# Four modulations computed as four strips of 32 columns, turned by sixteen small transfers

## The chip, the core and the metric

The kernel runs on one core of a Trainium2 chip. Such a core has five engines that run their own instruction streams and meet at semaphores: PE (matrix products; its weight loads are shown apart as PEld), DVE (VectorE), ACT (ScalarE), POOL (GpSimd) and SP (SyncE, which here only issues DMAs). Operands lie in SBUF (128 partitions); products come out in PSUM, used here as eight banks of 128 x 512 float32. The metric is the time of one execution in device microseconds, as a median over runs. All numbers are float32.

## What is computed

Two transformer layers, over 16 sequences of 256 tokens of width 256, with a conditioning vector per sequence. Each layer is self-attention, cross-attention to a context, and a feed-forward part:

```
layer 0 (16 heads of 64):
  adaln(x, g, b) = ln(x) * (1 + cond @ g) + cond @ b           # cond: 16 x 256
  x = attn(adaln(x, g1, b1)) + x                               # rotary positions
  x = cross_attn(adaln(x, g1, b1), ln(context)) + x
  x = gelu(adaln(x, g2, b2) @ ff_w1) @ ff_w2 + x
layer 1 (16 heads of 16):
  sh1, sc1, sh2, sc2, sh3, sc3 = split(silu(cond) @ Wmod, 6)
  x = x + attn(ln(x) * (1 + sc1) + sh1)
  x = x + cross_attn(ln(x) * (1 + sc2) + sh2, context)
  x = x + gelu((ln(x) * (1 + sc3) + sh3) @ W1) @ W2
```

A modulation is the pair of factors that scale and shift a normalised input: a product of 16 condition vectors (256 long) with a 256 x 512 weight, half of it the shift and half the scale. There are five: a1 (used by both attentions of layer 0), a2 (its feed-forward part), and b1, b2, b3 for the three parts of layer 1. The kernel wants each as a tile of 128 partitions (channel within a block of 128) by 2 (shift, scale) by 2 (block) by 16 (sequence), since it keeps activations with channels on partitions.

## The kernel before

The work is six phases (two attentions and a feed-forward part, for either layer) of 16 jobs, one per sequence. An attention job has two steps (s = 0, 1), a feed-forward job four. The order of instructions on every engine is the order in which the Python code emits them: nothing is rescheduled. A loop over all steps (from L901) emits, in each turn, pieces of the job at hand and of jobs ahead of it: normalisation three jobs ahead (`prepare_moments`, `prepare_norm`), the fetch of turned blocks two jobs ahead (`prepare_fetch`), the modulated input `hT` (`prepare_input`, L393 on ACT and L394 on POOL), the rotary products of the next step, and at the end of the turn the scores of the next step (`scores`, `stage_s`, L566).

PE products are mostly `product` (L80 to L82): four strips, each with 32 columns of weights and 32 partitions of output, one behind the other in the queue; the array holds the four side by side. In the trace a float32 product is two PE instructions.

One step of layer 0's cross-attention, with s = 1, matters below. DVE runs in this order: the moments of a later job at the end of the turn before (`context_moments`, its last instruction is L325); then `stage_t` twice (L587, sums of exponentials), `stage_turn` (L593), the rotary multiplications (L523, from PSUM) with `stage_t` between, `stage_reduce` (L600), and the additions of the finished output to x (`finish_folded`, L747 to L754, which read PSUM banks 4 and 5). POOL meanwhile runs `scale` (L624, four multiplications emitted at the end of step s = 0), `fold_inner` (L733), the rotary sums (L531). At the end of the turn PE computes the scores of the next step, first into banks 0 to 3, then into 4 to 7, so the second half has to wait until L754 has read bank 5.

There are two ways to compute a modulation. `modulation` (L180, used for a1 and a2) has the weights stationary: for each of 2 x 2 output blocks and each half of the inner dimension a product with 128 columns of weights and 16 columns streamed, whose result is already turned as it is wanted; five DVE instructions (`factors`, L173 to L177) make the factors from PSUM at once. For a2 this happens in job 2 of the cross-attention phase, at s = 1, between the first and second half of the rotary products. `modulation_turned` (L192, used for b1, b2, b3) has the 16 condition vectors stationary and streams 512 columns of weights, twice. The result has sequences on partitions. POOL clears a 32 x 512 tile (L202), ACT copies the result there (L203), DVE turns blocks of 32 x 32 (L205), SP moves the blocks to their partitions with four DMAs (L208), and `factors` runs later from SBUF. b1, b2 and b3 are made in jobs 2, 5 and 8 of layer 0's feed-forward phase at s = 3; their factors follow one job later (L931 to L933), at the head of step s = 3 of jobs 3, 6 and 9.

Of the kernel before, what the change touches and what calls it, by code (L numbers as in the profile page):

```python
# [10 lines left out]
F32 = mybir.dt.float32  # L11
# [5 lines left out]
P = 128  # L17
N = 256
D = 256
# [5 lines left out]
KC = D // P  # L25
# [18 lines left out]
def fast(ctx: ExitStack, tc: tile.TileContext, a: dict, out: bass.AP, flag):  # L44
# [4 lines left out]
    nc = tc.nc  # L49
    NB = a["x"].shape[0]  # L50
# [5 lines left out]
    work = ctx.enter_context(tc.tile_pool(name="work", bufs=2))  # L56
# [7 lines left out]
    def bank(i, *inner):  # L64

        flat = banks[:, i, :]
        if len(inner) == 1:
            return flat[:, 0 : inner[0]]
        return flat[:, 0 : inner[0] * inner[1]].rearrange("p (a n) -> p a n", n=inner[1])
# [34 lines left out]
    row_of, n_rows = {}, 0  # L104
# [20 lines left out]
    condT = const.tile([P, 2, KC, NB], F32, name="condT")  # L125
# [31 lines left out]
    def load_modulation(shift_w, scale_w, name, between=None):  # L157
        w = wpool.tile([P, KC, 2, D], F32, tag="mod", name=f"mod_{name}", bufs=1)
        nc.sync.dma_start(out=w[:, :, 0, :], in_=shift_w.rearrange("(c p) m -> p c m", p=P))
        if between is not None:  # L160
            between()
        nc.sync.dma_start(out=w[:, :, 1, :], in_=scale_w.rearrange("(c p) m -> p c m", p=P))
        return w

    def factors(name, pm, ln_w, ln_b, shift_b, scale_b):


        factor = stat.tile([P, KC, NB], F32, tag="fac", name=f"fac_{name}", bufs=4)
        addend = stat.tile([P, KC, NB], F32, tag="add", name=f"add_{name}", bufs=4)
        ln_w, ln_b, shift_b, scale_b = (  # L170
            cols[:, c : c + KC].unsqueeze(2).to_broadcast([P, KC, NB]) for c in (ln_w, ln_b, shift_b, scale_b)
        )
        nc.vector.tensor_tensor(addend, pm[:, 1], scale_b, ALU.add)  # L173
        nc.vector.scalar_tensor_tensor(factor, addend, 1.0, ln_w, ALU.add, ALU.mult)
        nc.vector.scalar_tensor_tensor(addend, addend, 1.0, ln_b, ALU.add, ALU.mult)
        nc.vector.tensor_tensor(addend, addend, shift_b, ALU.add)
        nc.vector.tensor_tensor(addend, pm[:, 0], addend, ALU.add)  # L177
        return factor, addend

    def modulation(name, at, w, *vectors):  # L180

        pm = bank(at, 2 * KC, NB).rearrange("p (s c) b -> p s c b", s=2)
        for s in range(2):
            for m in range(KC):
                for k in range(KC):
                    nc.tensor.matmul(
                        pm[:, s, m, :], w[:, k, s, m * P : (m + 1) * P], condT[:, 0, k, :],
                        start=(k == 0), stop=(k == KC - 1),
                    )
        return factors(name, pm, *vectors)  # L190

    def modulation_turned(name, at, w, *vectors):  # L192


        assert NB <= 32
        pm = bank(at, 2 * D)[0:NB]
        for k in range(KC):
            nc.tensor.matmul(
                pm, condT[:, 1, k, :], w[:, k].rearrange("p s m -> p (s m)"), start=(k == 0), stop=(k == KC - 1)
            )  # L200
        flat = work.tile([32, 2 * D], F32, tag="m0", name=f"flat_{name}")
        nc.gpsimd.memset(flat, 0.0)  # L202
        nc.scalar.copy(flat[0:NB], pm)  # L203
        blocks = work.tile([32, 2 * KC, 4, 32], F32, tag="m1", name=f"blocks_{name}")
        nc.vector.transpose(blocks.rearrange("p s q b -> p (s q b)"), flat)  # L205
        turned = work.tile([P, 2, KC, NB], F32, tag="inv", name=f"turned_{name}")
        for q in range(4):
            nc.sync.dma_start(  # L208
                out=turned[32 * q : 32 * q + 32].rearrange("p s c b -> p (s c) b"), in_=blocks[:, :, q, 0:NB]
            )  # L210
        return lambda: factors(name, turned, *vectors)

    def layer0_modulation(i, between=None):
        w = load_modulation(a[f"L0_xcond_b{i}_w"], a[f"L0_xcond_g{i}_w"], f"a{i}", between)
        return lambda at: modulation(
            f"a{i}", at, w,
            *(row_of[f"L0_xcond_{n}"][0] for n in (f"ln{i}_w", f"ln{i}_b", f"b{i}_b", f"g{i}_b")),
        )

    def layer1_modulation(i):  # L220
        at = 2 * (i - 1) * D
        w = load_modulation(
            a["L1_xcond_Wmod"][:, at : at + D], a["L1_xcond_Wmod"][:, at + D : at + 2 * D], f"b{i}"
        )
        c = row_of["L1_xcond_bmod"][0] + at // P
        return lambda at: modulation_turned(
            f"b{i}", at, w, row_of[f"L1_xcond_ln{i}_w"][0], row_of[f"L1_xcond_ln{i}_b"][0], c, c + KC
        )


# [559 lines left out]
    def count_outside():  # L790
# [10 lines left out]
    phases = [  # L801
        {"layer": 0, "kind": "attn", "cross": False, "load": lambda part: load_layer0_attention("sa", part, load_first),
         "mod_load": lambda: layer0_modulation(1, lambda: load_x(0))},
        {"layer": 0, "kind": "attn", "cross": True, "load": lambda part: load_layer0_attention("ca", part), "mod_load": None},
        {"layer": 0, "kind": "ffn", "cross": False, "mod_load": lambda: layer0_modulation(2),
         "load": lambda part: load_ffn("L0_xcond_ff_w1", "L0_xcond_ff_w2", "L0_xcond_ff_b1", "L0_xcond_ff_b2", "a", part)},
        {"layer": 1, "kind": "attn", "cross": False, "load": load_layer1_self, "mod_load": lambda: layer1_modulation(1)},
        {"layer": 1, "kind": "attn", "cross": True, "load": load_layer1_cross, "mod_load": lambda: layer1_modulation(2)},
        {"layer": 1, "kind": "ffn", "cross": False, "mod_load": lambda: layer1_modulation(3),
         "load": lambda part: load_ffn("L1_xcond_W1", "L1_xcond_W2", "L1_xcond_b1", "L1_xcond_b2", "b", part)},  # L810
    ]
# [18 lines left out]
    for p, ph in enumerate(phases):  # L830
        for b in range(NB):
            job = {"phase": ph, "p": p, "layer": ph["layer"], "kind": ph["kind"], "cross": ph["cross"], "b": b,
                   "key": f"{p}_{b}", "index": len(jobs), "qk": {}, "pr": {}, "turns": [], "raw": [], "parts": [], "halves": [],
                   "last": p == len(phases) - 1}
# [66 lines left out]
    for i, (j, s) in enumerate(steps):  # L901
        job = jobs[j]
        ffn, layer0 = job["kind"] == "ffn", job["layer"] == 0
# [17 lines left out]
            load_phase(job["p"] + 1, "first")  # L921
        if layer0 and not ffn and s == 1 and job["b"] == 2:
            make_mod = phases[job["p"] + 1]

        if ffn and layer0 and job["b"] in (2, 5, 8):
            at = phases[3 + job["b"] // 3]
# [4 lines left out]
        if ffn and layer0 and job["b"] in (3, 6, 9) and s == 3:  # L931
            at = phases[2 + job["b"] // 3]
# [84 lines left out]
        else:  # L1017
            then = attention(i + 1, 1)
            at = 4 * s
# [639 lines left out]
```

## Time and profile before

| | |
|---|---|
| median of 3 runs | 2198.77 us (2198.4 to 2199.13) |
| the profiled execution | 2198.01 us, of which its span is 2196.1 us |
| granted PE clock | 1.0 over the span |
| busy: PE, DVE, POOL, ACT | 2181.5, 1669.3, 1072.3, 838.2 us |
| sixteen PE instructions of a2 (L186) | 787.23 to 789.12 us |
| twelve PE instructions of b1, b2, b3 (L198), four each | the first starts at 1331.6, the last at 1414.4 us |

Busy time is the time in which an engine had an instruction of its own running; the rest of the span it waited. The chain of waits goes back from the last instruction to what released each, so a line of it is time that set the end. A timeline row gives start, length, engine, source line, operation and how many were merged; a bracket holds the idle time before it and what ended that. "SPq" rows are DMA issues: their length is the time that SP took to issue, not the transfer.

### The profile page before, as it was taken

The numbers are of one execution on the slowest core, as the hardware profiler recorded it, in microseconds if no ns is written. First come the engines' busy times: TensorE is split into PE (matmuls) and PEld (weight loads), VectorE is DVE, ScalarE is ACT, GpSimd is POOL, SyncE is SP. The second block draws the span as 40 slices with busy tenths as digits, with TensorE's granted clock in tenths as the row PEclk, the third lists the DMA queues.
The fourth block names the chain that finished last, engine by engine and source line by source line (L and its number), as shares of the span: only waits on it lengthen the run. The fifth ranks groups of instructions, "written<-read, shape, count | busy, mean of one in ns | idle before, by whom it ended". The sixth has DMA issues, their size and how long they took to land.

```text
span 2196.1 us, 110711 instructions
## 1 busy us (share of the span) xinstructions
PE 2181.5 (99%) x50469; PEld 1437.0 (65%) x50469; DVE 1669.3 (76%) x3119; ACT 838.2 (38%) x1306; POOL 1072.3 (49%) x1036
## 2 busy tenths in 40 slices
PE   9999999999999999999999999999999999999998
PEld 5656656656656666666666668787656656557887
DVE  6877777777787999989898876664777777777654
ACT  3323323323323333333333332334666666663222
POOL 3766566566557767676776752221323232222220
PEclk9999999999999999999999999999999999999999
DMA  6210111110132221212212033221222232223221
GB/s 192 49 37 23 27 37 23 28 37 22 31 89 64 71 60 35 59 41 45 56 37 60 23 74 87 52 45 29 62 43 42 52 95 59 62 52 85 61 62 37
DMA packets 307974, 117.77 MB, mean 54 GB/s; under 512 B 244308, under 2 KB 290728, under 8 KB 307368
## 3 DMA queue, kind: packets, MB, share of 16 engines
q1 hardware_dynamic: 307496, 110.61, 21.5%
q8 instruction: 396, 6.49, 1.3%
q14 instruction: 82, 0.67, 0.1%
HBM read 77.14 MB, written 33.29 MB: 50 GB/s over the span
## 4 chain that ended last, share of the span: by engine, by line
PE 92%; DVE 2%; POOL 2%; DMA 1%; issue 1%; SPq 1%; ACT 0%; DVEq 0%; POOLq 0%; ACTq 0%
PE banks L82 60%; PE banks L566 15%; PE banks L635 9%; PE banks L651 5%; PE banks L502 1%; PE banks L469 1%; POOL raw L624 1%; DVE m L523 1%; POOL qk L531 1%; DMA spread<-sums_seen 0%; POOL folded L733 0%; DMA turned<-blocks 0%; SPq L615 0%; DVE both L587 0%; SPq L350 0%
## 5 line engine op out<-in xcount | busy, mean ns | idle before, releaser
L578 ACT ACTIVATE pr<-banks 128x1024 f32<-128x1024 f32 x576 | 487.6, 938 | 414.3 <-PE banks L566 209.5
L531 POOL TENSOR_TENSOR qk<-m,m 128x512 f32<-128x512 f32 x256 | 347.0, 1376 | 292.5 <-DVE m L523 190.7
L523 DVE TENSOR_TENSOR m<-banks,rope 128x512 f32<-128x512 f32 x512 | 324.1, 679 | 87.1 <-POOL qk L531 83.2
L587 DVE TENSOR_TENSOR both<-pr 128x512 f32<-128x512 f32 x256 | 227.9, 903 | 101.4 <-ACT pr L578 101.2
L642 ACT COPY raw<-banks 128x512 f32<-128x512 f32 x128 | 75.0, 587 | 468.5 <-PE banks L635 461.8
L566 PE MATMUL banks<-qk 32*64 32x256 f32 x8192 | 241.3, 378 | 2.9 <-DVE x L750 2.0
L635 PE MATMUL banks<-pr,v 128*32 128x256 f32 x4096 | 233.2, 379 | 0.0
L566 PEld LDWEIGHTS banks<-qk 32*64 32x64 f32 x8192 | 185.4, 131 | 62.9 <-issue 23.0
L701 ACT ACTIVATE g<-banks,cols 128x256 f32<-128x256 f32 x256 | 106.9, 470 | 288.3 <-PE banks L82 274.9
L635 PEld LDWEIGHTS banks<-pr,v 128*32 128x32 f32 x4096 | 133.1, 110 | 88.5 <-ACT pr L578 0.7
L624 POOL TENSOR_TENSOR raw<-raw,spread 128x512 f32<-128x512 f32 x128 | 164.6, 1318 | 25.4 <-DMA spread<-sums_seen 23.2
L82 PE MATMUL banks<-folded_w,folded 128*32 128x128 f32 x5856 | 175.1, 273 | 0.4 <-POOL folded L733 0.3
L82 PEld LDWEIGHTS banks<-folded_w,folded 128*32 128x32 f32 x5856 | 162.5, 110 | 1.5 <-POOL folded L733 1.5
L593 DVE STREAM_TRANSPOSE squares<-both 128x1024 f32<-128x1024 f32 x128 | 159.4, 1246 | 4.4
L600 DVE TENSOR_REDUCE rows<-squares 128x32 f32<-128x1024 f32 x128 | 155.5, 1215 | 2.2
L686 POOL TENSOR_TENSOR oT<-oT,spread 128x256 f32<-128x256 f32 x64 | 45.7, 735 | 209.9 <-DVE spread L685 209.9
L327 POOL TENSOR_TENSOR rstd<-ve,neg_half 128x2 f32<-128x2 f32 x95 | 75.1, 790 | 144.0 <-DVE ve L325 140.7
L651 PE MATMUL banks<-pr,wide_v 128*32 128x256 f32 x2048 | 134.4, 379 | 1.1 <-ACT pr L578 1.1
L82 PE MATMUL banks<-hT,wk_sa 128*32 128x256 f32 x2048 | 134.9, 381 | 0.1
L420 POOL TENSOR_TENSOR x<-x,bo_b 128x256 f32<-128x256 f32 x96 | 73.1, 781 | 126.1 <-DVE xh L335 126.1
L82 PE MATMUL banks<-hT,wq_sa 128*32 128x256 f32 x2048 | 134.0, 379 | 0.0
L82 PE MATMUL banks<-hT,wq_ca 128*32 128x256 f32 x2048 | 133.9, 379 | 0.0
(157 smaller groups left out, 3669.6 us busy)
## 6 DMA issues: line engine op xcount, KB each, us to landing
turned<-blocks SPq DMA_DIRECT2D x380, 64.0 KB
fetched<-turned SPq DMA_DIRECT2D x380, 64.0 KB
spread<-sums_seen SPq DMA_DIRECT2D x128, 128.0 KB
x<-in_x SPq DMA_DIRECT2D x16, 256.0 KB
fetched_c<-turned_c SPq DMA_DIRECT2D x64, 64.0 KB
cT<-in_ctx_turned SPq DMA_DIRECT2D x16, 256.0 KB
out<-x SPq DMA_DIRECT2D x16, 256.0 KB
ctx<-in_ctx SPq DMA_DIRECT2D x16, 192.0 KB
```

The costliest lines, as they stand in the source:

```text
L82: nc.tensor.matmul(out[cut], lhsT[:, cut], rhs, start=start, stop=stop)
L523: nc.vector.tensor_tensor(m, pq, rope[:, s : s + 1, :].to_broadcast([P, 2, N]), ALU.mult)
L531: nc.gpsimd.tensor_tensor(r, x, y, (ALU.subtract, ALU.add)[out])
L566: nc.tensor.matmul(banks[64 * g : 64 * g + 64, at + h, t * N : (t + 1) * N], lhs, rhs, start=(half == 0), stop=(half == 1 or job["layer"] ...
L578: nc.scalar.activation(pr[:, one], sc[:, one], AF.Exp, scale=0.125 if job["layer"] == 0 else 0.25)
L587: nc.vector.tensor_tensor(job["both"][:, 2 * p : 2 * p + 2, :], pr[:, :, 0, :], pr[:, :, 1, :], ALU.add)
L593: nc.vector.transpose(job["squares"].rearrange("p b k -> p (b k)"), job.pop("both").rearrange("p h n -> p (h n)"))
L600: nc.vector.tensor_reduce(job["rows"][:, u, :], job.pop("squares"), AX.X, ALU.add)
L624: nc.gpsimd.tensor_tensor(part, part, spread[:, u : u + 1, :].to_broadcast([P, 2, N]), ALU.mult)
L635: nc.tensor.matmul(o[32 * h : 32 * h + 32, half, :], v[:, t, col : col + 32], prs[h // 2][:, h % 2, t, :], start=(t == 0), stop=(t == NT - 1),
L651: nc.tensor.matmul(o[32 * h : 32 * h + 32], v[:, t, 4 * c + h, 32 * e : 32 * e + 32], prs[h // 2][:, h % 2, t, :], start=(t == 0), stop=(t ...
L701: nc.scalar.activation(g[:, c, :], ph[:, c, :], AF.Gelu, bias=column(w["b1"], 2 * u + c))
```

## The change

a2, b1, b2 and b3 all go through `modulation_turned`; only a1 keeps `modulation`. The condition vectors are 16 columns of weights, as they were. Instead of streaming 512 columns in one go, the product is cut into four strips g of 128 columns: strip g uses array columns 32g onward and puts its 16 rows on partitions 32g to 32g + 15 of one bank. The copy by ACT is now 128 x 128 instead of 16 x 512, and takes along the partitions that no strip wrote; the clearing by POOL is gone. The tiles of the copy and of the turned blocks have places of their own. The turn on DVE is 128 x 128 instead of 32 x 512. Since the blocks now lie on four groups of partitions, sixteen DMAs of 32 x 16 elements take the place of four of 32 x 64. For a2 the factors are no longer made at once: they follow one job later, in job 3 of the cross-attention phase, at the head of step s = 1, ahead of `stage_t`, and read SBUF where they read PSUM.

```
-    def modulation_turned(name, at, w, *vectors):
+    def modulation_turned(name, of, at, w, *vectors):
         assert NB <= 32
-        pm = bank(at, 2 * D)[0:NB]
+        pm = bank(at, P)
         for k in range(KC):
-            nc.tensor.matmul(
-                pm, condT[:, 1, k, :], w[:, k].rearrange("p s m -> p (s m)"), start=(k == 0), stop=(k == KC - 1)
-            )
-        flat = work.tile([32, 2 * D], F32, tag="m0", name=f"flat_{name}")
-        nc.gpsimd.memset(flat, 0.0)
-        nc.scalar.copy(flat[0:NB], pm)
-        blocks = work.tile([32, 2 * KC, 4, 32], F32, tag="m1", name=f"blocks_{name}")
-        nc.vector.transpose(blocks.rearrange("p s q b -> p (s q b)"), flat)
+            for g in range(4):
+                nc.tensor.matmul(
+                    pm[32 * g : 32 * g + NB], condT[:, of, k, :], w[:, k, g // KC, g % KC * P : (g % KC + 1) * P],
+                    start=(k == 0), stop=(k == KC - 1),
+                )
+        flat = work.tile([P, P], F32, tag="flat", bufs=1, name=f"flat_{name}")
+        nc.scalar.copy(flat, pm)
+        blocks = work.tile([P, 4, 32], F32, tag="flat_turned", bufs=1, name=f"blocks_{name}")
+        nc.vector.transpose(blocks.rearrange("p q b -> p (q b)"), flat)
         turned = work.tile([P, 2, KC, NB], F32, tag="inv", name=f"turned_{name}")
         for q in range(4):
-            nc.sync.dma_start(
-                out=turned[32 * q : 32 * q + 32].rearrange("p s c b -> p (s c) b"), in_=blocks[:, :, q, 0:NB]
-            )
+            for g in range(4):
+                nc.sync.dma_start(
+                    out=turned[32 * q : 32 * q + 32, g // KC, g % KC, :], in_=blocks[32 * g : 32 * g + 32, q, 0:NB]
+                )
         return lambda: factors(name, turned, *vectors)

     def layer0_modulation(i, between=None):
...
-        return lambda at: modulation(
+        make = modulation if i == 1 else lambda name, *rest: modulation_turned(name, 0, *rest)
+        return lambda at: make(
...
         return lambda at: modulation_turned(
-            f"b{i}", at, w, ...
+            f"b{i}", 1, at, w, ...
...
         if layer0 and not ffn and s == 1 and job["b"] == 2:
             make_mod = phases[job["p"] + 1]
+        if layer0 and not ffn and s == 1 and job["b"] == 3:
+            late_mod = phases[job["p"] + 1]
+            if late_mod["kind"] == "ffn":
+                late_mod["mod"] = late_mod["mod"]()
```

More of the change, by code (lines that the diff above doesn't have):

```diff
@@ L226, in layer1_modulation @@
         return lambda at: modulation_turned(
-            f"b{i}", at, w, row_of[f"L1_xcond_ln{i}_w"][0], row_of[f"L1_xcond_ln{i}_b"][0], c, c + KC
+            f"b{i}", 1, at, w, row_of[f"L1_xcond_ln{i}_w"][0], row_of[f"L1_xcond_ln{i}_b"][0], c, c + KC
         )
```

## The prediction

> **What bounds the kernel now.** I read the page's first and fourth parts, then the chain of waits around each modulation, then the timeline of DVE and POOL at the two steps of the cross-attention phase that the change touches, then the DMA issues.
>
> ```profile
> PE 2181.5 (99%) x50469; PEld 1437.0 (65%) x50469; DVE 1669.3 (76%) x3119; ACT 838.2 (38%) x1306; POOL 1072.3 (49%) x1036
> PE 92%; DVE 2%; POOL 2%; DMA 1%; issue 1%; SPq 1%; ACT 0%; DVEq 0%; POOLq 0%; ACTq 0%
> ```
>
> PE is the bound: 92% of the chain, busy 99%. A microsecond saved on PE is a microsecond of the end, as long as the other engines keep up. Whether they do is a matter of place: DVE's 76% is an average.
>
> ```profile
> 762.17 0.43 DVE x L754
> 762.61 0.04 issue
> 762.65 1.98 PE banks L566 x62
> ...
> 787.23 1.89 PE banks L186 x16
> ...
> 1372.49 1.10 PE banks L198 x3
> 1373.60 0.23 PE banks L82 x5
> 1373.82 0.38 PE banks L198
> 1374.21 39.06 PE banks L82 x1038
> ```
>
> These are pieces of the chain of waits. At 762 us it leaves PE: the second half of the scores (L566) waits for DVE's last addition to x (L754). So in a cross-attention step DVE can set the end, and how much room it has there decides part of this change. The other lines are the modulations' PE time.
>
> ```profile
> 790.12 0.19 DVE L174 SCALAR_TENSOR_TENSOR fac_a<-add_a,cols 128x32 f32<-128x32 f32 x1
> 790.13 2.56 POOL L531 TENSOR_TENSOR qk<-m,m 128x512 f32<-128x512 f32 x2 [0.72 <-DVE add_a L173]
> 790.35 1.16 DVE L175 SCALAR_TENSOR_TENSOR add_a<-add_a,cols 128x32 f32<-128x32 f32 x1
> 791.54 1.21 DVE L176 TENSOR_TENSOR add_a<-add_a,cols 128x32 f32<-128x32 f32 x1
> ...
> 819.52 4.98 POOL L624 TENSOR_TENSOR raw<-raw,spread 128x512 f32<-128x512 f32 x4 [0.85 <-DMA spread<-sums_seen]
> 821.59 0.47 DVE L325 TENSOR_SCALAR ve_c<-mv_c 128x2 f32<-128x2 f32 x1
> 823.35 3.39 DVE L587 TENSOR_TENSOR both<-pr 128x512 f32<-128x512 f32 x2 [1.30 <-ACT pr L578]
> 824.58 4.55 POOL L733 TENSOR_TENSOR folded<-raw,raw 128x512 f32<-128x512 f32 x3
> ...
> 840.97 0.42 DVE L754 TENSOR_TENSOR x<-banks,x 128x256 f32<-128x256 f32 x1
> ```
>
> The first four rows are the factors of a2 as they run now. The same tiny operation takes 0.19 us before POOL has started and about 1.2 us beside it: each held one ends when a POOL instruction ends. The next four are where the changed kernel puts those five instructions: between L325 and L587 of job 3, in the midst of seven POOL instructions.
>
> **PE, what is removed.** a2: the chain has PE score groups at 779.80 and 801.41 around it, 21.61 us apart; one job later, without a modulation, at 820.25 and 839.84, 19.59 apart. So a2 costs 2.02 us of PE. b2: L198 holds the chain from 1372.49 to 1374.21, 1.72 us, four instructions 0.43 apart (the five L82 in between are the tail of the work before; I let them run beside it).
>
> **PE, what is added.** Each modulation becomes 2 x 4 products of 128 columns streamed in strips of 32 columns, 16 PE instructions. The nearest row is finish_folded's, with the same array strips and 128 columns: 224 in 6.11 us, 27.3 ns each, so 0.44 us. PE saves 2.02 - 0.44 = 1.58 for a2 and 1.72 - 0.44 = 1.28 for each of three: 5.42 us. The bound from the other side is strips that do not run side by side, because only 16 of their 32 columns are used: then 16 x 4 x 27.3 ns = 1.75 us, no better than now, and the saving is 0.2 us.
>
> **a2's factors, moved.** In job 2, DVE loses the five instructions (789.91 to 792.97, 3.06 us with their waits on POOL) and gets one block turn of 128 x 128, which I put at 0.2 us: turning 128 x 256 takes 0.38 (L345). It waits for ACT's copy, but ACT is idle from 785.6 to 793.7 and PE is done 2 us before DVE arrives. PE's step is 0.44 longer than one without modulation, DVE's at most 0.4; no wait.
>
> In job 3 the five come at 822.06, when L325 ends. All five now read two SBUF tiles (before, L173 and L177 read PSUM). DVE was idle to 823.35 anyway, waiting for the exponentials, so in free air (5 x 0.22 = 1.1 us, as b1's factors take at 1345.6) they would cost nothing. But POOL runs L624 to 824.50 and then three L733, and DVE's L587, which also reads two SBUF tiles, alternates with them. By the held rows each of the five lets one POOL instruction pass: two to 824.5, three more to 824.58 + 3 x 1.28 = 828.4. Then the two L587 at 0.68 each (their median) end at 829.8. Before, they ended at 826.74. DVE is 3.06 us later. Lower bound: nothing, if all five slip through together at one gap. Upper: each held by a POOL instruction of 1.8 us (the longest L733), 9.0 - 1.3 of idle time: 7.7.
>
> Does anything absorb it? From 826.77 to L754's end at 841.39 DVE is idle once, 1.17 us before L523 at 832.79, for a rotary sum of POOL that itself follows an earlier L523, so that gap moves along. The second half of the scores starts 1.82 us after 839.84, at 841.66: 0.27 us of room. Everything behind L587 on DVE (turn, rotary products, sums, additions) goes late together, POOL's rotary sums with it, and PE then waits 3.06 - 0.27 = 2.8 us before the second half. It is lost for good, since PE has no idle time later to make it up.
>
> [...]
>
> **b1 to b3, beside PE.** ACT's copy and DVE's turn get shorter (0.57 and 0.70 us now) and POOL's clearing goes (0.51, off the path): no cost, hidden behind PE.
>
> SP: sixteen issues for four.
>
> ```profile
> L208 SPq DMA_DIRECT2D turned_b<-blocks_b x12: 591/602/1608, 1334.9 to 1418.3; - x12
> L360 SPq DMA_DIRECT2D fetched<-turned x380: 302/418/2126, 35.0 to 2147.0; - x190
> ```
>
> Four took 2.56 us at b1, 0.64 each. Bounds for sixteen: 16 x 0.46 = 7.4 us (fetched, four in 1.82) and 16 x 0.89 = 14.2 us (b2's four took 3.55, one of them 1.6 us). I take L208's 0.64, nearest in ends and element size, and one long issue: 11.3 us. Starting at 1333.75 (1.1 us earlier than now, since PE and ACT are), with some 1.9 us to land (from an issue of sums at 811.81 + 0.41 to the release of its reader at 813.99), the blocks are there at 1346.9. The factors would start at 1344.4 (1345.61 less PE's 1.28): DVE waits 2.5 us. Behind it in DVE's queue is `fold_inner`, whose first result PE wants at 1351.07 - 1.28 = 1349.8; factors 1.1 and one fold 0.7 must fit ahead of that, so the blocks may land as late as 1348.0. They do, with 1.1 us to spare. If that cover goes, PE waits microsecond for microsecond, three times.
>
> Also moved back on SP at b1 are five weight and bias loads (needed a phase later) and the fetch for job 5: issued by 1350.5 instead of 1342.9, landed by 1352.4, where ACT and POOL want it at 1347.3. Both wait 5 us; behind ACT's are the three gelus of job 4. Their banks are wanted again eight banks later, about 15 us on, and the folds that read them at 1360: hidden. At a2, SP issues from 788.5 to 800 while its queue is empty (780.3 to 804.3): no cost.
>
> **Sum.** -5.42 + 2.8 = -2.6 us. The profiled execution took 2198.01, so it would take 2195.4; the median of the runs shown is 0.76 above it, so the forecast is 2196.2, on the median's scale. Its own range: strips 0.2 dearer each (+0.8), the wait of a2 from 1.5 to 4.2: 2194.9 to 2198.4.
>
> **Rival 1, the factors of a2 slip through.** If POOL's instructions leave DVE gaps to run in, PE does not wait and the whole -5.42 stands: 2193.3. For it: L174 got through in 0.19. In some steps (955 to 994 us) DVE reaches L754 half a microsecond earlier. Against: POOL's seven instructions there stand in a row with gaps under 0.1 us, and two L325 just before are held as well (0.47 us for 0.17).
>
> **Rival 2, slower: the sixteen issues take too long.** Place: SP behind b1, b2, b3. Price: beyond 16 issues in 12.3 us (0.77 each) PE waits for what goes over, at `fold_inner`, three times. From there it first eats the gain; at 0.91 each (14.6 us, three times 2.3 = 6.9) the kernel is 4.4 us slower, and at 1.0 (16 us, three times 3.7) the time is 2196.2 + 11.1 = 2207.3. For it: one quartet of three had 0.89, and about one issue in twelve of the SP queue takes over 0.95 us. Against: two quartets at 0.64, and the plain fetches at 0.46.
>
> **Rival 3, the change does not do what it says on PE.** Strips of 16 active columns run one after another: PE saves 0.2 us in all and the 2.8 us remain: 2198.77 - 0.2 + 2.8 = 2201.4. Against: L82 does the same with 32 active columns in the same strips.
>
> **How the numbers follow.** About 0.2% (4.4 us) is what a measurement of this kernel can tell from no change. Forecast 0.50 (within). Rival 1 0.33 (faster). Rival 2 0.12, of which 0.11 past the point of 0.2% slower. Rival 3 0.05 (within; 0.01 with more loss). So faster 0.34, with what the forecast's low end adds; slower 0.12; within 0.54. The range reaches from rival 1 with 0.5 us of spread, 2192.8, to rival 3, 2201.4; left out is most of rival 2.
>
> **What would show it.** PE's sixteen instructions at each modulation in about 0.44 us (rival 3: 1.75). Score groups around a2 20.0 us apart instead of 21.6. In the next job, s = 1: five factor instructions of which at least three take about 1.2 us, L587 ending 3 us later against the score group before, L754 releasing L566 in the chain of waits, and a step of 22.4 us instead of 19.6 (rival 1: 19.6). At b1 to b3: SP's sixteen issues in 7 to 12 us; DVE idle before L173 up to 2.5 us; the distance between the jobs' gelus 13.5 us instead of 14.7, and no wait of PE for a fold (rival 2: there is one). I am wrong first if POOL and DVE share more kindly than the held rows say.

## The result, and the profile after

| | before | changed |
|---|---|---|
| median, 22 runs each | 2198.37 us (2195.86 to 2199.67) | 2195.40 us (2194.12 to 2198.99) |
| the profiled execution | 2198.01 us, span 2196.1 | 2198.64 us, span 2196.8 |

The ratio is 0.9987, with a 95% interval of 0.9981 to 0.9993: 3.0 us less, between 1.5 and 4.2. Forecast were 2196.2 us and a difference of 2.6.

The profiled execution is one of the longest of the changed kernel's 22, so the two profiles can't be compared by their ends. By stages they can. I used PE's score groups (L569 in the new numbering, three more than before) as marks:

| stretch | before | changed | difference |
|---|---|---|---|
| start to the first score group | 24.26 | 28.14 | +3.88 |
| to the group ahead of a2 | 755.54 | 754.88 | -0.66 |
| a2 and the two jobs behind it, four groups | 78.87 | 79.25 | +0.38 |
| the feed-forward phase with b1 to b3 | 246.49 | 243.99 | -2.50 |
| all the rest | 1090.9 | 1090.5 | -0.4 |

The change emits no instruction in the start, and the kernel before can start as late (the last section). The third and fourth rows are the change: -2.1 us in this pair of profiles.

The first and the fourth part of the page of the changed kernel:

```profile
PE 2180.7 (99%) x50505; PEld 1431.6 (65%) x50505; DVE 1660.6 (76%) x3120; ACT 837.5 (38%) x1307; POOL 1071.6 (49%) x1033
PE 91%; DVE 3%; POOL 2%; DMA 1%; issue 1%; SPq 0%; ACT 0%; DVEq 0%; POOLq 0%; ACTq 0%
```

PE is still the bound, but a point of its share of the chain has gone to DVE. Where, the chain of waits of the same kernel tells (start, length, engine, tile, line):

```profile
783.02 3.64 PE banks L569 x128
...
790.45 0.44 PE banks L199 x16
...
803.05 3.69 PE banks L569 x128
...
822.09 0.85 DVE ve L328
...
824.09 0.19 DVE add_a L173
824.30 1.17 DVE fac_a L174
825.49 0.20 DVE add_a L175
825.72 1.16 DVE add_a L176
826.90 1.20 DVE add_a L177
828.11 2.35 DVE both L590 x2
...
844.64 0.43 DVE x L757
845.12 1.98 PE banks L569 x62
...
862.27 3.64 PE banks L569 x128
```

The modulation (L199) takes 0.44 us and the groups around it stand 20.02 us apart, 21.61 before. Then, from 813 to 845 us, the chain leaves PE altogether: it runs through the five factors, of which three take 1.16 to 1.20 us, through L590 and on to L757, which releases the second half of a score group. That half starts late by some 2 us, and so the next group comes 20.78 us after this one, where the kernel before has 18.83.

At b1 to b3 the issues by SP, in the view of their source line (min, median, max in ns):

```profile
L210 SPq DMA_DIRECT2D turned_b<-blocks_b x48: 518/589/1663, 1337.1 to 1428.5; - x48
L210 SPq DMA_DIRECT2D turned_a<-blocks_a x16: 555/589/1197, 794.2 to 804.4; - x16
...
  DVE add_b L173: 8.1, 3
```

Sixteen took 12.7, 12.2 and 12.1 us at b1, b2 and b3. DVE waited 2.6, 2.2 and 3.4 us for them, and PE for none of the folds behind. But PE does wait in this phase, once, where it did not before. The timeline, with idle time in brackets:

```profile
1358.93 0.60 ACT L396 ACTIVATE hT<-fetched,add_a,fac_a 128x256 f32<-128x256 f32 x1 [8.88 <-DMA fetched<-turned]
1359.03 0.56 POOL L397 TENSOR_SCALAR hT<-fetched,fac_a,add_a 128x256 f32<-128x256 f32 x1 [15.03 <-DMA fetched<-turned]
1359.05 1.99 PEld L82 LDWEIGHTS banks<-folded_w,folded 128*32 128x32 f32 x73 [0.83 <-issue]
```

ACT and POOL get the fetch for job 5 only at 1358.9, and at the same moment PE goes on after 0.83 us without work. "issue" means that the profile shows nothing that PE waited for. Whether the first two rows cause the third is settled in the last experiment: they do not.

### The profile page after: what moved, and what is told of

Read it like the earlier page. It is cut to its first block, busy times and chain, and to the rows that moved or that the text cites. A ratio compares the mean times of both kernels' runs of the same rounds, so it can differ in the third digit from the quotient of the medians.

```text
span 2196.8 us, 110836 instructions
## 1 busy us (share of the span) xinstructions
PE 2180.7 (99%) x50505; PEld 1431.6 (65%) x50505; DVE 1660.6 (76%) x3120; ACT 837.5 (38%) x1307; POOL 1071.6 (49%) x1033
## 4 chain that ended last, share of the span: by engine, by line
PE 91%; DVE 3%; POOL 2%; DMA 1%; issue 1%; SPq 0%; ACT 0%; DVEq 0%; POOLq 0%; ACTq 0%
PE banks L82 59%; PE banks L569 15%; PE banks L638 9%; PE banks L654 5%; PE banks L505 1%; PE banks L472 1%; DVE m L526 1%; POOL raw L627 1%; POOL qk L534 1%; DMA spread<-sums_seen 0%; POOL folded L736 0%; DMA sums_seen<-inv 0%; DVE both L590 0%; DVE rows L603 0%; DVE squares L596 0%
## 5 line engine op out<-in xcount | busy, mean ns | idle before, releaser
L526 DVE TENSOR_TENSOR m<-banks,rope 128x512 f32<-128x512 f32 x512 | 324.2, 679 | 86.4 <-POOL qk L534 80.8
L590 DVE TENSOR_TENSOR both<-pr 128x512 f32<-128x512 f32 x256 | 222.7, 884 | 107.7 <-ACT pr L581 107.4
L569 PE MATMUL banks<-qk 32*64 32x256 f32 x8192 | 241.4, 378 | 4.0 <-DVE x L753 2.8
L569 PEld LDWEIGHTS banks<-qk 32*64 32x64 f32 x8192 | 184.9, 131 | 64.6 <-issue 28.7
L627 POOL TENSOR_TENSOR raw<-raw,spread 128x512 f32<-128x512 f32 x128 | 162.8, 1304 | 19.0 <-DMA spread<-sums_seen 17.7
```

Of the source, the lines that this page charges most:

```text
L526: nc.vector.tensor_tensor(m, pq, rope[:, s : s + 1, :].to_broadcast([P, 2, N]), ALU.mult)
L569: nc.tensor.matmul(banks[64 * g : 64 * g + 64, at + h, t * N : (t + 1) * N], lhs, rhs, start=(half == 0), stop=(half == 1 or job["layer"] ...
L590: nc.vector.tensor_tensor(job["both"][:, 2 * p : 2 * p + 2, :], pr[:, :, 0, :], pr[:, :, 1, :], ALU.add)
L627: nc.gpsimd.tensor_tensor(part, part, spread[:, u : u + 1, :].to_broadcast([P, 2, N]), ALU.mult)
```

## The experiments

The theory ahead of them: PE saves what was forecast, a2's factors give 1.5 to 2 us of it back because DVE's two-input instructions alternate with POOL's, and the sixteen issues stay covered. The rivals: the wait in job 3 comes from something else than the shared inputs; the issues cost time already; the difference is only scatter of the start.

**e1: the factors of a2 in a quiet place.** The five instructions are emitted in job 4, s = 0, behind the first rotary product.

```
-            if late_mod["kind"] == "ffn":
-                late_mod["mod"] = late_mod["mod"]()
...
             rotary(then, 0, 0)
+            if s == 0 and job["b"] == 4 and job["p"] == 1:
+                phases[2]["mod"] = phases[2]["mod"]()
             stage_t(job, 2 * s + 1, 0)
```

> The changed kernel, but a2's five factor instructions stand in job 4 at s = 0, behind the first pair of rotary products, where the trace of before shows POOL idle for 5.6 us. Theory (DVE and POOL exclude each other there, and PE pays): each factor instruction takes about 0.2 us; the scores of job 3, s = 1, are no longer held up, the distance to the next score group falls from 20.8 to 18.9 us, and the time from 2195.4 to about 2193.4 us (5.0 to 5.4 us below the kernel before). Rival (DVE has no room for five more instructions anywhere in this phase): about 1 to 2 us of PE waiting show up one job later, and the time stays near 2195.4.

Measured: 2194.41 us against 2198.92 (ratio 0.9977, with its 95% interval 0.9968 to 0.9987), 4.5 us less, where 5.0 to 5.4 were expected. Its chain of waits stays on PE through the same place:

```profile
820.01 3.64 PE banks L569 x128
...
839.60 3.64 PE banks L569 x128
843.24 1.05 PE banks L505 x16
...
858.43 3.64 PE banks L569 x128
```

839.60 to 858.43 is 18.83, as before the change: the wait is gone. So it was the place of the five instructions, not the copy, the transfers or the strips.

**e2 and e3: the two halves of the change alone.** Strips for b1 to b3 with a2 as it was, and strips for a2 alone, with its late factors in job 3 (`modulation_rows` is the function that b1 to b3 had before). The first edit is that of b1 to b3 alone, which leaves out the late call too.

```
-        make = modulation if i == 1 else lambda name, *rest: modulation_turned(name, 0, *rest)
+        make = modulation
```

> Only b1, b2 and b3 as four strips; a2 as before. Theory: three times 1.28 us less of PE, no wait of PE behind the sixteen transfers although DVE idles some 2.7 us ahead of each group of factors: 3.8 us below the kernel before, 13.5 us between the gelus around a modulation instead of 14.7. Rival (the sixteen issues cost PE something): less than 3 us of gain, and PE waits for a fold.

Measured: 2196.91 against 2198.92 (0.9988, 0.9979 to 0.9997), 2.0 us less, between 0.7 and 4.6, where 3.8 were expected. The groups around a2 stand 21.61 apart again. The rival's wait for a fold is not there, but PE's other wait in the feed-forward phase, that of the changed kernel, is (0.76 us at 1356 us).

```
-        return lambda at: modulation_turned(
+        return lambda at: modulation_rows(
```

> Only a2 as four strips with its factors late; b1 to b3 as before. Theory: PE saves 1.58 us in job 2 and waits 1.95 us in job 3, so the time is 0.4 us above the kernel before, which a measurement does not tell from it; score groups 20.0 us apart around a2, and 20.8 in the next job but one step. Rival (the wait in job 3 is a chance of that one profile): 1.6 us below.

Measured: 2197.47 against 2198.92 (0.9996, 0.9987 to 1.0005). The step of a2 is 20.02, and the interval that held 18.83 is 20.27: 1.59 won and 1.44 lost again. The median alone, 1.45 us less, is nearer to the rival, but its interval reaches from 2.9 less to 1.1 more; that the wait is there is read from the trace. PE has no wait behind the loads of the feed-forward phase. By the traces a2 gives almost nothing, and b1 to b3 most of the difference.

**e4 and e5, what holds DVE: five instructions with one input, then five with two.** On top of the first experiment's kernel, five more instructions at the head of job 3, s = 1, that compute nothing of use, so each such kernel does more work than the reference asks. First turns, with one SBUF input; in the second kernel the last line of the edit is `nc.vector.tensor_tensor(t, cols[:, 0:32], cols[:, 32:64], ALU.add)`, with two.

```
             then = attention(i + 1, 0)
+            if s == 1 and job["b"] == 3 and job["p"] == 1:
+                for n in range(5):
+                    t = work.tile([P, 32], F32, tag="probe", bufs=1, name=f"probe_{n}")
+                    nc.vector.transpose(t, cols[:, 0:32])
             stage_t(job, 2 * s, 0)
```

> As e1_quiet, and five turns of 128 x 32 (one SBUF input each, results unused) stand on DVE where the changed kernel has a2's factors, ahead of the sums of job 3, s = 1. Theory (it is the second SBUF input that makes an instruction wait for POOL): each turn takes 0.1 to 0.2 us beside POOL, all five fit in the 1.3 us in which DVE waits for the exponentials, and the step stays as in e1_quiet (18.9 us). Rival (any five DVE instructions there are late): the step is 20 us or more, as in the changed kernel.

> As e4_one_input, but the five extra DVE instructions add two columns tables of 128 x 32, both in SBUF, instead of turning one; they read no DMA's result. Theory (two SBUF inputs wait for POOL): each held one takes about 1.2 us, PE waits 1.4 to 2 us, score groups behind job 3, s = 1, are 20.3 to 20.8 us apart instead of 18.83, and the time is 1.5 to 2 us above e4_one_input. Rival (in the changed kernel it was the wait for the sixteen transfers, or the five dispatches): 18.83 us as with the turns.

Measured: 2195.16 against 2198.92 (0.9981, 0.9972 to 0.9990) with one input, and 2195.19 against 2197.82 (0.9988, 0.9979 to 0.9997) with two. Against the kernel of the first experiment neither median is far enough off to tell, but the traces are plain. DVE's timeline with one input:

```profile
822.04 1.18 DVE L980 STREAM_TRANSPOSE probe<-cols 128x32 f32<-128x32 f32 x5
823.25 0.69 DVE L590 TENSOR_TENSOR both<-pr 128x512 f32<-128x512 f32 x1
...
826.83 1.25 DVE L526 TENSOR_TENSOR m<-banks,rope 128x512 f32<-128x512 f32 x2
```

and with two:

```profile
820.30 5.24 DVE L980 TENSOR_TENSOR probe<-cols 128x32 f32<-128x32 f32 x5
825.46 1.39 DVE L590 TENSOR_TENSOR both<-pr 128x512 f32<-128x512 f32 x2
```

Five in 1.18 us against five in 5.24, of the same size, in the same place, beside the same POOL instructions (L627, then L736). The two also differ in the operation, but that is not it. L526 above is the operation of the second kernel with one of its inputs in PSUM, and two of it run in 1.25 us beside POOL's L736, as fast as elsewhere (0.68 us each is the mean of the line):

```profile
823.41 4.61 POOL L736 TENSOR_TENSOR folded<-raw,raw 128x512 f32<-128x512 f32 x3
```

With one input the next interval of PE is 18.83, with two it is 20.32, 1.49 more: the wait of the changed kernel, made with instructions that have nothing to do with a modulation. In these two runs what holds the DVE instructions is the second SBUF input beside POOL: 0.24 us each with one, 1.05 with two. One SBUF input is not free in every operation, though: just ahead of the five turns two small TENSOR_SCALAR (L328, 128 x 2) took 0.62 and 0.47 us, and the shortest of that line take 0.17. Why they are held was not tried. Nor do the medians show the 1.5 to 2 us between the two kernels that were expected (3.8 and 2.6 us below the kernel before).

**e6: the weight loads one job later.** Of the first experiment's kernel, the loads of the next phase's weights and biases (SP) are issued in job 4 of the feed-forward phase, not in job 3.

```
-        if s == 1 and job["b"] == (3 if ffn else 1) and more:
+        if s == 1 and job["b"] == (4 if ffn else 1) and more:
```

> As e1_quiet, and the five weight and bias loads of the next phase are issued in job 4 of layer 0's feed-forward phase instead of job 3, so that they no longer stand on SP between b1's sixteen issues and the fetch for job 5. Theory (issues and loads together make the fetch late, ACT waits for it ahead of three gelus, and PE then waits 0.8 us for a bank that a late gelu still holds): ACT's wait falls from 8.9 to some 5 us, PE's gap of 0.8 us between two L82 at about 1355 is gone, and the time is 0.8 to 0.9 us below e1_quiet, near 2193.6 and 2.4 per mille below the kernel before. Rival (the sixteen issues alone are enough to hold it): the gap stays.

Measured: 2192.10 against 2197.82 (0.9977, 0.9968 to 0.9986), 5.7 us less, the lowest median here, and 3.1 us below the kernel with two inputs, which ran beside it. Its ratio is the same as the first experiment's, so the medians do not tell these two apart; the traces do. PE's wait is gone, and the feed-forward phase takes 243.04 us, 0.93 less than in the first experiment. The cause that was expected, a late gelu that holds a bank, is not the one (see e11).

**e7: half as many issues again.** On top of that, eight more small transfers ahead of the sixteen at each of b1, b2 and b3, into a tile that nobody reads.

```
+        if of == 1:
+            spare = work.tile([P, 2, KC, NB], F32, tag="spare", bufs=1, name=f"spare_{name}")
+            for q in range(4):
+                for g in range(2):
+                    nc.sync.dma_start(
+                        out=spare[32 * q : 32 * q + 32, g // KC, g % KC, :], in_=blocks[32 * g : 32 * g + 32, q, 0:NB]
+                    )
```

> As e6_loads_later, with eight more transfers of the same kind into an unused tile ahead of the sixteen, at b1, b2 and b3. Theory (the cover of b1 to b3 is 1.1 us more than the sixteen need, and beyond it PE waits microsecond for microsecond): 8 x 0.63 = 5.1 us later, PE waits 4.0 us at each of three, 12 us in all. Rival (fewer waits: the folds are wanted later than I think): under 5 us in all.

Measured: 2208.98 against 2197.82 (1.0048, 1.0032 to 1.0063), 11.2 us more than before the change and 16.9 more than without the eight. The waits in the feed-forward phase:

```profile
DVE add_b L173 <- DMA turned_b<-blocks_b: 21.8, 3, 7.7
...
PEld banks L82 <- DVE folded L743: 10.6, 3, 4.0
...
PEld banks L82 <- issue: 5.0, 8, 3.4
```

DVE waits 21.8 us for the blocks where the kernel without the eight waits 5.1, and now PE waits for the folds behind: three times, 10.6 us in all (3.4, 4.0 and 3.3, against 7.2, 7.7 and 7.0 of DVE). The difference is 3.7 us each time, so PE begins to wait when DVE has waited 3.7 us. The prediction put that point at 2.5 + 1.1 = 3.6. In the changed kernel, with 2.6, 2.2 and 3.4, the margin is 1.1, 1.5 and 0.4 us.

The phase grew by more, 16.5 us. Another 3.4 us are a wait at 1361 us for nothing that the profile shows. And with two of these four waits the granted clock falls (stretch, its length, PE's busy time and instructions, granted clock, share of the DMA engines, GB/s):

```profile
1364.50:1368.00 3.50, 3.11 (x32) 0.51 0.42 70
...
1400.00:1404.50 4.50, 3.67 (x92) 0.73 0.49 94
```

The trace's records have it at 0.5 from 1364.5 to 1367.9 and from 1402.1 to 1405.5 us, that is from 0.4 us ahead of the end of the wait at 1361 us (PE goes on at 1364.89), and from 1.2 us behind the second wait for a fold. The seven short waits for "issue" lie in the first of the two. If PE works at half the pace under a record of 0.5, it loses there half of 3.0 and of 3.4 us, by estimate 1.5 and 1.7. With these 3.2 the sum is 17.2 by the waits of the weight loads, and 15.3 by the time that PE itself stood still (9.2 and 2.9); the 16.5 lie between.

**e8 to e10: is the start part of it?** Two more profiles of the kernel before and one of the changed one, without an edit.

> The kernel before once more, for its profile. In the profile shown of it the first scores start at 24.3 us, in those of the changed kernel and of the first four experiments at 27.3 to 28.1. Theory (the start depends on when the first transfers land, in any kernel): this one can start as late as 27 us or later, and its span follows. Rival (the change makes the start later): 24.3 us again.

> The changed kernel once more, for its profile. Theory: what the change does repeats (score groups 20.02 us apart around a2, a wait of 1.4 to 2 us behind job 3, one gap of some 0.8 us in the feed-forward phase), while the start (28.1 us to the first scores in the first profile) moves freely between 24 and 28 us. Rival (the change makes the start later): again 27 us or more.

> The kernel before a third time, for its profile. Theory: its start, 24.3 and 26.0 us so far, moves as freely and can be 27 us or more. Rival: it stays at 26 us or less.

Measured: the kernel before took 2196.18 and 2202.19 us, with its first score group at 26.03 and 28.40 us (24.26 in its first profile); the changed one 2195.65, with 28.48. The kernel before can start as late as any. In this profile of the changed kernel the interval of job 3 is 20.32, 1.49 over 18.83.

**e11: the fetch ahead of the loads.** What was left is PE's wait at 1358 us. Of the first experiment's kernel, SP issues the fetch for job 5 ahead of the weight loads, in the same step.

```
             if s == 1 and after is not None:
                 prepare_fetch(after)
+            if s == 1 and layer0 and job["b"] == 3:
+                load_phase(job["p"] + 1, "early")
```

> The kernel of e1 with the weight and bias loads of the next phase issued in the same step, but behind the fetch for job 5 instead of ahead of it. Two theories of PE's wait of 0.8 us near 1355 us, which stands in the changed kernel and in all variants that load there. Theory D (data): PE waits because the fetch for job 5 lands late, and ACT and POOL with it. Then the fetch, no longer behind the loads, lands some 2 us after its issue, ACT and POOL wait 4 to 6 us instead of 7.4 and 13.6, and PE's wait is gone. Theory P (program): the loads' transfers hold up the transfer that brings PE its next 256 instructions. In the changed kernel and in e1, e2, e4 and e5 PE went on 1.3 to 1.5 us after such a transfer had landed, and that transfer had started only after PE had run 370 to 397 instructions since the one before, instead of the usual 256. Then ACT and POOL wait less here too, but PE still has a wait of 0.4 to 1 us within the 6 us behind the loads, ending 1.3 to 1.5 us after a late program transfer. Theory P allows no wait only if the program transfer happens to start before the loads' traffic, after at most some 350 instructions.

Measured: one execution, 2195.44 us beside 2198.67. The timeline, of ACT, POOL and PE's weight loads:

```profile
1349.61 0.60 ACT L396 ACTIVATE hT<-fetched,add_a,fac_a 128x256 f32<-128x256 f32 x1 [3.20 <-DMA fetched<-turned]
...
1349.69 2.07 POOL L397 TENSOR_SCALAR hT<-fetched,fac_a,add_a 128x256 f32<-128x256 f32 x1 [9.35 <-DMA fetched<-turned]
...
1355.73 1.99 PEld L82 LDWEIGHTS banks<-folded_w,folded 128*32 128x32 f32 x73 [1.16 <-issue]
```

ACT and POOL are served five microseconds before PE stops (at 1354.57), and PE still stops, for longer (1.16 us; POOL still waited 9.35, where 4 to 6 were expected). The late data are not the cause. Now the DMA view of this kernel, first of the stretch 1346.2 to 1353.3 us, then of 1353.3 to 1355 us (queue, kind: packets, MB, share of the 16 engines):

```profile
q1 hardware_dynamic: 994, 1.51, 71.1%
...
q1 hardware_dynamic: 1995, 0.30, 105.8%
q8 instruction: 1, 0.02, 3.9%
```

Queue 8, of kind "instruction", moves 397 packets of 16384 bytes over the whole execution of the changed kernel, and its 101,010 instructions of PE and PEld divided by 397 are 254 each, one packet for about 256 instructions. In the records of the single packets, the median distance between two of them is 256 to 260 PE instructions in the thirteen traces. I read them as PE's program; what they hold no trace shows. While the loads (1.3 MB) keep the DMA engines busy, from 1347 on (99.2% from 1349.9 to 1353.3 us), no such packet comes. It starts at 1353.36, after PE has run 404 instructions, lands at 1354.41, and PE goes on 1.32 us later. The same in the other kernels:

| kernel | PE instructions since the last packet of queue 8 | it landed at | PE goes on | later by |
|---|---|---|---|---|
| changed | 396 | 1357.60 | 1359.05 | 1.45 |
| changed, second profile (e9) | 420 | 1354.91 | 1356.17 | 1.26 |
| e1, a2's factors in a quiet place | 374 | 1353.51 | 1354.96 | 1.45 |
| e2, b1 to b3 alone | 397 | 1355.29 | 1356.59 | 1.30 |
| e4, one input | 380 | 1353.70 | 1355.11 | 1.41 |
| e5, two inputs | 370 | 1353.77 | 1355.25 | 1.48 |
| e7, half as many issues again | 462 | 1363.47 | 1364.89 | 1.42 |
| e11, fetch ahead of the loads | 404 | 1354.41 | 1355.73 | 1.32 |
| e6, loads a job later | 346 | 1355.24 | no wait | |
| before | 375 | 1344.76 | no wait | |

The reading that fits them all, though no trace shows it directly: PE had run out of program, and the loads stood in the way of its transfer. The kernel before had a late packet too, since the same loads went out some 9 us earlier, but it landed at 1344.76, just when PE had gone over (at 1344.4) to products with 256 columns. These use up instructions more slowly: in the changed kernel's timeline 122 in 6.86 us, 17.8 per us, against 52 in 1.66 us, 31.3 per us, with 128 columns. In e6 the late packet meets the same passage, 10 us on. Where the sixteen issues have pushed the loads back by those 9 us, the packet lands in the midst of products with 128 columns. That this difference decides is read from the traces and was not tried by itself. That it is not the data of job 5, e11 shows; that it is the packet is read from the time between its landing and PE's return, 1.26 to 1.48 us in all eight traces that have the wait. The 3.4 us at 1361 us in e7 fit it too: PE went on 1.42 us after the landing of a packet that came after 462 instructions.

## Why the prediction was right, and where it was not

**PE's part** was exact where it was measured: 0.44 us for each of the four modulations, 20.02 between the groups around a2 (20.0 forecast), 13.46 between the gelus around b1 to b3 (13.5 forecast). One term was over-sized: b1 cost 1.35 us before, not 1.72. I took b2's 1.72 for all three. So PE saved 0.91 + 2 x 1.28 + 1.58 = 5.05 us, not 5.42.

**The wait behind a2's factors** was forecast with its place and its cause, and both held: three of the five take about 1.2 us, L757 releases the second half of the scores, and a quiet place makes the wait vanish. In e4 and e5 an instruction beside POOL took 0.2 us with one input and 1.05 on average with two; that the second SBUF input decides, the rows that the prediction read had not shown. The size was off: 2.8 us forecast, 1.95, 1.44 and 1.49 measured in three traces (changed, a2 alone, the changed once more). The step that failed is "DVE is 3.06 us later". It assumed that POOL starts its seven instructions as long ahead of the score group as in the kernel before. There L624 started at 819.52, 0.7 us ahead of the group at 820.25; in the changed kernel the same series started at 820.41, 1.4 us ahead of the group at 821.8. POOL was through earlier, so DVE came 2.1 us late rather than 3.06. The wait goes with that lead: 1.95 us at 1.4, and 1.44 to 1.49 at 1.9 to 2.1 (e3, e5 and e9). The profile that the prediction read was itself the exception: in the two later ones of the kernel before POOL is 1.8 and 1.7 us ahead of the group, and L754 ends 0.55 us earlier, so the room was about 0.8 us there and not 0.27. I also named the wrong interval for it: the wait falls between the halves of a score group and lengthens the interval behind, 20.78 for 18.83, and not the one that I said would read 22.4, which is 19.58 as before.

**The sixteen issues** took 12.1 to 12.7 us for 11.3, and DVE waited 2.7 us on average for 2.5. The cover held. It ends when DVE has waited 3.7 us, as the eight more issues show, and at b3 only 0.4 us of it were left. Rival 2 was the right mechanism at a point that this kernel does not quite reach. Past that point its price, microsecond for microsecond, is too low: with two of the four waits in e7 the granted clock was recorded at 0.5 for 3.4 us.

**"Hidden"**, said of the loads (four in the trace, five in the prediction's words) and the fetch that SP issues later, is the step that failed in kind. ACT and POOL did wait, 8.9 and 15.0 us where I had 5, since the fetch took 5 us to land behind the loads (issued by 1353.94, read at 1358.93) and not 2; and that wait is indeed hidden. What I did not price is the loads' own traffic: moved by some 9 us, it lay ahead of a packet of queue 8 that came after 396 instructions of PE, and PE lost 0.84 us. Nothing in the prediction looks at that queue, although a line of the page shows it ("q8 instruction").

**The sum**, with what was measured: -5.05 + 0.84 + 1.95 = -2.3 in the changed kernel's profile (-2.1 by the stages), and -2.7 with the 1.49 of its second profile. The medians say -3.0, from -4.2 to -1.5. The forecast of -2.6 is as near as it is because a wait over-sized by about 1 us stood against a saving over-sized by 0.4 and a wait of 0.8 that was not in it.

**The rivals.** Rival 1 (the factors slip through) falls: the wait is in every trace that has the factors there. Its time, 2193.3, is near what the kernel with the factors in a quiet place took. Rival 3 (the strips run one after another) falls: 0.44 us and not 1.75.

## What to carry to other kernels

Before a tiny DVE instruction is moved, look at what POOL does in the new place: with two SBUF inputs most of them took 1.2 us for 0.2 here, about as long as one POOL instruction beside them (1.25 for L627), while turns with one took 0.2 in the same place. When a change makes SP issue more, follow everything queued behind it to the place where it now lands, bulk loads above all: by the reading of e11, 1.3 MB of them kept PE from its program here, which showed only as an idle PE that waited for "issue" (0.83 us in the changed kernel, 1.16 in e11) after the queue of kind "instruction" had been silent for 396 and 404 instructions of PE. Both were repaired here by moving a few lines. By the traces that took back 1.4 to 2.0 and 0.9 us, nearly as much as the change alone had won (3.0).

## What the runs showed of the hardware that was not expected

**The packets of queue 8 can come late.** There is one of 16 KB for about every 256 instructions of PE (397 for 101,010 in the changed kernel). In eight traces a packet that came only after 370 to 462 instructions, behind the loads, was followed by an idle PE, which went on 1.26 to 1.48 us after it had landed. There are such waits at other places too: at 1782 to 1790 us e3 has one of 1.29 us, e4 one of 1.02 and e10, a profile of the kernel before, one of 1.79, each ending 1.32 to 1.42 us after the landing of a packet that came after 404 to 452 instructions. Not every late packet costs something: the changed kernel has one there after 424 instructions, and no wait. So part of the scatter between executions is probably of this origin; that was not tested.

**The start has two paces, and the fast one begins with the records of the granted clock.** The sixteen PE instructions of a1 (L186; weight loads, min, median, max in ns) in the kernel before, in the changed one, and in the third profile of the kernel before, which has both paces for its two modulations a1 and a2 in one row:

```profile
L186 PEld LDWEIGHTS banks<-condT,mod_a x32: 186/192/290, 6.2 to 788.8; 128*128 128x128 f32 x32
```

```profile
L186 PEld LDWEIGHTS banks<-condT,mod_a x16: 333/333/392, 6.6 to 9.8; 128*128 128x128 f32 x16
```

```profile
L186 PEld LDWEIGHTS banks<-condT,mod_a x32: 186/262/394, 6.7 to 791.5; 128*128 128x128 f32 x32
```

The same instruction takes some 190 ns at one time and 333 at another. The trace's records of the granted clock begin at 6.35 us in the first of these, at 14.85 in the second and at 15.18 in the third, and in all thirteen traces the weight loads turn to the fast pace where they begin. A window of the profile counts time without a record as 1.00, so it does not show this. In e8, a profile of the kernel before, the slow pace has a record of its own (columns as in e7):

```profile
6.40:9.70 3.30, 2.95 (x24) 1.00 0.84 277
9.70:13.10 3.40, 3.40 (x24) 0.50 1.04 393
13.10:16.50 3.40, 3.40 (x72) 1.00 1.08 349
```

Most loads of 128 x 128 take 192 ns in the first stretch, and both of the second take 337. The first score group goes with these records: it stands at 24.3 us in the first profile, at 26.0 in e8, and at 26.7 to 28.5 in the eleven others, whose records begin at 12.3 to 15.4 us. The expectation of e8 had put it down to the first transfers; what the traces show is the pace of the weight loads: 337 ns under a record of 0.50 (e8), 333 where there is no record yet (changed), 192 under one of 1.00. That the stretch without a record has a clock of 0.50 too is my estimate from these three numbers.

Why the records begin late in some executions stays open, and so does whether the change has a part in it: in two of the three profiles of the kernel before they begin at 6.3 or 6.4 us, and in none of the ten with the change or a part of it. Nor is it shown how much of a late start reaches the end: in e8 the first score group is 1.8 us later than in the first profile, and the span 1.8 us shorter. In the pair of profiles above, the start's 3.9 us are why they differ by +0.7 us where the medians differ by -3.0.
